# A graph layer on one core: six kept units fetched row by row by SyncE, ten by POOL

## The chip, the cores and the metric

The kernel runs on one core of one Trainium2 chip. Times are device microseconds of one execution; a kernel's time is the median of its runs. The trace is of one more execution, taken by the hardware profiler. Engines are named as in the profile: PE is the matrix engine (TensorE), PEld its weight load, DVE the vector engine, ACT the scalar engine, POOL GpSimd, and SP SyncE, which here only issues transfers (SPq is its queue of instructions).

## The reference

There are 6250 nodes with 256 features and 206,250 edges, sorted by their target `dst`. All is fp32.

```python
h = relu(layernorm(x))
e = relu(raw @ W_e1.T + b_e1) @ W_e2.T + b_e2            # raw: 64 numbers an edge
edge_emb = (e * (clip(polarity, 0, 1) + 0.01)) @ W_le.T + b_le
msg = relu(h[src] + edge_emb)                            # a row of h for each edge
aggr = segment_sum(msg, dst)
g = (h + aggr) @ W_g1.T + b_g1
out = x + relu(layernorm(g) * ln_g + ln_b) @ W_g2.T + b_g2
```

## The kernel before, in words

The edges are padded and cut into 806 units of 256 edges. Two units are a block; twelve units (`GU`) are a group of 3072 edges, of which there are 68. A buffer `hg` or `hx` (the latter eight lie in another tensor's memory) holds the 256 gathered rows of one unit: 128 partitions, two halves of 256 features.

The rows of the layer's input with its bias are first written to DRAM as `hb_d`. POOL gathers from there: one indirect DMA (L722) fetches 128 rows by the numbers in a column of `src_s`, two of them make a unit. Units are gathered in the order of a list, `order`, as buffers come free. There are 25 buffers (`HG`).

A loop runs over the units. For each unit `edge_part` lets TensorE form the edge products (L372); DVE multiplies them by the polarity and adds the gathered rows in place (`whole`, L755), and ACT applies the ReLU in place (L766). After the twelfth unit of a group three things follow: the first layer of edges to come (L338, fed by `raw` tiles that SP loads at L320), then the sums (`add_pairs`, L806: 96 matmuls that add up the rows of a group by target, using a selection matrix `sel`), and then `keep`: ACT and DVE copy the sum into a tile `ms` (L824, L825). A unit's buffer is free once its matmuls at L806 are done, and then POOL may gather into it the unit that comes 25 further on.

The first 24 units (`KEPT`, groups 0 and 1) are different. Their edge products are made at the start, while the layer's input is still being made, and kept in tiles `msg`. Units 0 to 7 (`RAW`) get rows straight from x, early. For units 8 to 23, the kernel before puts the gather into `order` ahead of unit 42 + 36 n, which is every third group, at its middle. One unit later, `whole_kept` (L770 to L787) multiplies, adds and applies the ReLU, and the product's buffer is free again at once, in the middle of the group. When a kept group's last unit is whole, `ready` names it and its sums are formed at the next group's end.

SP is a queue in program order too. A group's work on it: `raw` loads (L320), then `rows_out`, which loads four row numbers into SP's registers (L905) and stores the four strips of `ms` at these rows of `sum_d` in DRAM (L910); the load of `xt` (L240); the load of `ab`, the finished sums of 128 nodes (L943), which DVE adds to the nodes' rows some units later (L946); a clearing of rows of `sum_d` (L899) and the store of an output (L235). `soon(n, fn)` puts such a step n units later.

Of the kernel before, what the change touches and what calls it, by code (L numbers as in the profile page):

```python
# [10 lines left out]
I32 = mybir.dt.int32  # L11
# [6 lines left out]
P = 128  # L18
N = 6250
# [9 lines left out]
S = 4  # L29
L = 6  # L30
# [6 lines left out]
NP = -(-NB // 2)  # L37
# [3 lines left out]
LEAD = 22  # L41
BANKS = 8
RAW = 8
HG = 17 + RAW
GU = 2 * L
KEPT = 2 * GU
EVERY = 6 * L
SEEDS = 3
FILL = 3
FEW = KEPT // 4  # L50
# [23 lines left out]
def groups_of(w):  # L74
    return [g for g in range(NG) if w in windows_of(g)]
# [22 lines left out]


@with_exitstack  # L100
def gnn_kernel(ctx: ExitStack, tc: tile.TileContext, x, src_c, dst_c, dst_r, pol_c, raw_t, w_e1t, w_e2,
               w_let, w_g1t, w_g2t, vec_c, row_v, x_t, out):
    nc = tc.nc

# [2 lines left out]
    hb_d = dram.tile([N, D], F32, name="hb_d")  # L107
# [38 lines left out]
    def apart_from(ins, *others):  # L146

        for other in others:
            if other is not None:
                tc.declare_no_dep(ins.ins, other.ins, reason="what is waited for has waited for it")  # L150
# [100 lines left out]
    with fast:  # L251
# [8 lines left out]
        raw, fours, sel, e1, hg, msg, ms = {}, {}, {}, {}, {}, {}, {}  # L260
# [101 lines left out]
        def plain(u):  # L362

            return u < LEAD and u % 3 == 1
# [32 lines left out]
        def seed(u):  # L397

            if KEPT <= u < NU and u not in seeds:
                bank = ps.take(True, True)  # L400
                bank.held = True
                a = nc.scalar.activation(bank.tile, bc_s, AF.Copy)  # L402
                if bank.reader is not None:
                    apart_from(a, bank.writer)
                seeds[u] = bank
# [34 lines left out]
        def forward(u, between=lambda: None):  # L440

            edge_part(u)
            between()
            turn_of(u)
# [50 lines left out]
        with tc.tile_pool(name="p1", bufs=4) as p1, tc.tile_pool(name="p1x", bufs=11) as p1x:  # L495
# [76 lines left out]
            for k in range(len(parts) + 1):  # L572
# [24 lines left out]
                for _ in range((k > 0) + (k > 2 and k % 3 > 0)):  # L597
                    u = next(units, None)
                    if u is not None:
                        forward(u)  # L600
                if k in lists:
                    t, src = lists[k]
# [93 lines left out]
        with tc.tile_pool(name="hg", bufs=1) as hg_p, tc.tile_pool(name="ms", bufs=4) as ms_p, \  # L696
# [5 lines left out]
            free = deque((hg_p.tile([P, 2, D], F32, name=f"hg{i}"), ()) for i in range(RAW, HG))  # L702
            fetched = RAW
            order = list(range(KEPT, NU))
            beside = {}
            for r in range(RAW, KEPT):
                i = KEPT + EVERY * (r - RAW) + EVERY // 2
                beside[i] = r
                order.insert(order.index(i), r)
            order = deque(order)  # L710
# [5 lines left out]
            def gathers():  # L716

                while free and order:
                    u = order.popleft()
                    hg[u], formerly[u] = free.popleft()  # L720
                    for i in range(2):
                        g = nc.gpsimd.indirect_dma_start(  # L722
                            out=hg[u][:, i, :], out_offset=None, in_=hb_d,
                            in_offset=bass.IndirectOffsetOnAxis(ap=src_s[:, 2 * u + i:2 * u + i + 1], axis=0))
                        apart_from(g, *formerly[u])

            def select(g):

                return [(g, lambda k=k: rows_of_blocks(g, k)) for k in range(0, len(blocks_of(g)), 2)]
# [12 lines left out]
            def piece():  # L742

                due_now = [s for s in steps if s[0] <= now][:1]
                if due_now:
                    steps.remove(due_now[0])
                    due_now[0][1]()
                elif rest:
                    rest.popleft()[1]()

            def whole(u):

                bank = seeds.pop(u)
                for i in range(2):
                    product = nc.vector.scalar_tensor_tensor(  # L755
                        hg[u][:, i, :], bank.tile[:, i, :], pol_s[:, 2 * u + i:2 * u + i + 1], hg[u][:, i, :],
                        op0=ALU.mult, op1=ALU.add)
                    apart_from(product, *formerly[u])
                    users.setdefault(u, []).append(product)
                    if u == NU - 1:  # L760
                        nc.scalar.activation(hg[u][:, i, :], hg[u][:, i, :], AF.Relu)
                bank.reader = product
                bank.held = False
                ps.touch(bank)
                if u < NU - 1:
                    done[u] = product, nc.scalar.activation(hg[u], hg[u], AF.Relu)  # L766
                    apart_from(done[u][1], *formerly[u])
                    users[u].append(done[u][1])

            def whole_kept(u):  # L770

                m = msg[u]
                if u < RAW:
                    nc.vector.tensor_add(hg[u], hg[u], ble_b.rearrange("p (o d) -> p o d", o=1).to_broadcast([P, 2, D]))
                if plain(u):
                    nc.vector.tensor_add(m, m, bc_s)
                for i in range(2):
                    nc.vector.scalar_tensor_tensor(m[:, i, :], m[:, i, :], pol_s[:, 2 * u + i:2 * u + i + 1],  # L778
                                                   hg[u][:, i, :], op0=ALU.mult, op1=ALU.add)
                nc.scalar.activation(m, m, AF.Relu)  # L780
                free.append((hg[u], ()))
                hg[u] = m
                u += 1
                if u % (2 * L) == 0:
                    g = u // (2 * L) - 1
                    rest.extend(select(g))
                    ready.append(g)  # L787

# [92 lines left out]
            late = {}  # L881
            steps = deque()
            rest = deque()
            ready, fillers = [], []
            left = {w: set(groups_of(w)) for w in range(NW) if groups_of(w)[-1] < FAR}
            held_back = sorted(left)[-FILL:]
# [2 lines left out]
            moves = {}  # L889
# [192 lines left out]
            def due():  # L1082

                fns = todo.pop(now, deque())
                if fns and not (KEPT <= now < NF * GU and now % GU in QUIET):
                    fns.popleft()()
                if fns:
                    todo.setdefault(now + 1, deque()).extendleft(reversed(fns))

            gathers()  # L1090
            sums = add_pairs

# [26 lines left out]
            raw_at = {}  # L1119
# [12 lines left out]
            for u in range(LEAD, NU):  # L1132
                now = u

                def between():

                    nonlocal made
                    for n in range(1, SEEDS + 1):
                        if u + n <= u // GU * GU + GU:
                            seed(u + n)  # L1140
                    piece()
                    if KEPT <= u:
                        whole(u)
                        made += 1
                    r = raw_at.get(u, beside.get(u - 1))
                    if r is not None:
                        whole_kept(r)

                forward(u, between)
                for n in range(1, SEEDS + 1):  # L1150
                    seed(u + n)
                gathers()
                due()
                for fn in moves.pop(now, []):
                    fn()
                if len(rest) + len(steps) > 4:
                    piece()
                if u == NU - 24:
                    for w in range(NW):
                        if groups_of(w)[-1] == NG - 1:  # L1160
                            late[w] = node_work(w, True)
                if u == LEAD + 60:
                    flag = nc.values_load(bad_i[0:1, 0:1], min_val=0, max_val=4 * P)
            while todo:
                now = min(todo)
                for fn in todo.pop(now):
                    fn()
            assert not moves
            while steps:
                steps.popleft()[1]()  # L1170
            (_, _, h_rows, h_one, h_normed, h_two, h_three, _), = ending[-2]
# [205 lines left out]
```

## Time and profile before

| | us |
|---|---|
| median of three runs | 3826.62 |
| lowest, highest | 3807.94, 3829.58 |
| the profiled execution | 3820.48 |
| its span, first to last instruction | 3818.7 |
| mean granted TensorE clock | 0.789 |
| busy: PE, POOL, DVE, ACT | 3030.0, 1563.9, 1315.3, 1295.4 |
| idle of ACT ahead of L824, which copies a sum | 1791.0 |

A row of groups gives the line, engine, operation and tiles, the count, then the busy time and the mean of one in ns, and then the idle time of the engine ahead of them with what ended most of it. A row of waits gives who waited, for whom, then the time in total, how often, and the longest. A row of the timeline gives start and length, engine, line, operation, count, and in brackets the idle time ahead and its releaser. A row that begins with a stretch of time (`720.00:730.00`) gives what each engine did in it. A row of one line's instructions gives the count, then shortest, median and longest in ns, and the first and last start.

Over the span the picture repeats with the group, 57 us on average: TensorE is busy without a gap for about half of it, and the other half goes with the sums.

### The profile page before, as it was taken

The page shows a single profiled execution, that of the slowest core. Times are in us where ns is not written, and L with a number is a line of the kernel's source. Part 1 is how long each engine was busy: PE and PEld are TensorE (multiplying, and loading weights), DVE is VectorE, ACT ScalarE, POOL GpSimd, SP SyncE. Part 2 cuts the span into 40 slices and gives each one's busy share as a digit, 9 for nine tenths or more (in the row PEclk, how much of TensorE's full clock was granted, in tenths as well). Part 3 has the DMA queues.
Part 4 walks back from the last instruction along what each step waited for, and adds up shares of the span by engine and source line. Part 5 has one row for each costly group of instructions (what it writes and reads, how often), then busy time and mean ns, then how long its engine had stood idle before and what let it go on. Part 6 is the DMA issues. An engine that isn't in the chain of part 4 may idle for free.

```text
span 3818.7 us, 51854 instructions
## 1 busy us (share of the span) xinstructions
PE 3030.0 (79%) x19998; PEld 1840.7 (48%) x19998; DVE 1315.3 (34%) x2970; ACT 1295.4 (34%) x2408; POOL 1563.9 (41%) x1674
## 2 busy tenths in 40 slices
PE   8477787788787787788787788787787888787788
PEld 5344454454455454454455455455454455455446
DVE  5343233242233232233233233233233343233234
ACT  5243233243233232333233233233242343233234
POOL 7434434424434434434433434433434434433431
PEclk9787787787787787787787787787787787787788
DMA  7322222223223222223322222322222222222321
GB/s 252 103 74 81 83 85 84 84 74 92 87 79 89 85 81 79 83 79 90 90 82 77 86 80 83 95 82 73 89 82 88 83 82 81 86 82 79 88 76 44
DMA packets 143718, 331.53 MB, mean 87 GB/s; under 512 B 36000, under 2 KB 71417, under 8 KB 142713
## 3 DMA queue, kind: packets, MB, share of 16 engines
q0 software_dynamic: 77376, 211.39, 19.2%
q1 hardware_dynamic: 64788, 113.47, 9.7%
q8 instruction: 159, 2.61, 0.3%
q10 hardware_dynamic: 1300, 3.29, 0.3%
q14 instruction: 95, 0.77, 0.1%
HBM read 306.25 MB, written 34.08 MB: 89 GB/s over the span
## 4 chain that ended last, share of the span: by engine, by line
PE 66%; another core or an unknown queue 16%; issue 14%; DVE 2%; ACT 2%; DMA 1%; POOL 0%; DVEq 0%; ACTq 0%; POOLq 0%
PE pz L372 41%; PE pz L806 13%; PE pz L338 9%; PE pz L188 1%; PE pz L227 1%; PE pz L173 1%; DVE hg L755 1%; ACT hg L766 1%; ACT pz L402 0%; PE pz L214 0%; ACT ms L824 0%; DVE sel L737 0%; DVE msg L778 0%; DMA hg<-hb_d,src_s 0%
## 5 line engine op out<-in xcount | busy, mean ns | idle before, releaser
L372 PE MATMUL pz<-wc_s,e 128*128 128x256 f32 x6448 | 1857.5, 439 | 407.0 <-issue 331.4
L372 PEld LDWEIGHTS pz<-wc_s,e 128*128 128x128 f32 x6448 | 1387.7, 220 | 861.4 <-issue 589.3
L722 POOL DMA_INDIRECT hg<-hb_d,src_s x1096 | 1038.3, 947 | 1394.3 <-PE pz L806 856.6
L722 POOL DMA_INDIRECT hx<-hb_d,src_s x500 | 473.6, 947 | 789.5 <-PE pz L806 461.3
L825 DVE TENSOR_TENSOR ms<-ms,pz 128x256 f32<-128x256 f32 x68 | 28.7, 421 | 1842.9 <-remote 715.0
L806 PE MATMUL pz<-hg,sel 64*32 64x256 f32 x4312 | 520.6, 406 | 174.7 <-issue 147.1
L824 ACT ACTIVATE ms<-pz 128x256 f32<-128x256 f32 x68 | 26.0, 383 | 1791.0 <-remote 1700.4
L755 DVE SCALAR_TENSOR_TENSOR hg<-pz,pol_s,hg 128x256 f32<-128x256 f32 x1078 | 467.4, 479 | 352.9 <-PE pz L372 90.2
L766 ACT ACTIVATE hg<-hg 128x512 f32<-128x512 f32 x538 | 337.7, 628 | 401.3 <-DVE hg L755 351.8
L402 ACT ACTIVATE pz<-bc_s 128x512 f32<-128x512 f32 x782 | 453.2, 586 | 0.0
L806 PEld LDWEIGHTS pz<-hg,sel 64*32 64x32 f32 x4312 | 164.8, 108 | 487.9 <-issue 457.8
L338 PE MATMUL pz<-raw,we_s 64*32 64x512 f32 x6448 | 377.5, 596 | 7.8 <-DVE hg L755 5.0
L350 DVE TENSOR_SCALAR e<-pz,vecs 128x512 f32<-128x512 f32 x395 | 296.3, 751 | 106.3 <-remote 24.6
L806 PE MATMUL pz<-hx,sel 64*32 64x256 f32 x1944 | 263.4, 407 | 82.5 <-issue 71.7
L353 ACT ACTIVATE e<-pz,vecs 128x512 f32<-128x512 f32 x411 | 272.6, 683 | 96.3 <-PE pz L338 40.5
L755 DVE SCALAR_TENSOR_TENSOR hx<-pz,pol_s,hx 128x256 f32<-128x256 f32 x486 | 211.8, 479 | 161.0 <-PE pz L372 49.7
L338 PEld LDWEIGHTS pz<-raw,we_s 64*32 64x32 f32 x6448 | 116.4, 107 | 226.5 <-issue 127.0
L766 ACT ACTIVATE hx<-hx 128x512 f32<-128x512 f32 x243 | 152.6, 628 | 189.9 <-DVE hx L755 165.8
L806 PEld LDWEIGHTS pz<-hx,sel 64*32 64x32 f32 x1944 | 81.1, 108 | 230.1 <-issue 217.3
L173 PE MATMUL pz<-ident,stb 128*128 128x128 f32 x84 | 25.6, 403 | 84.5 <-issue 63.9
L737 DVE SCALAR_TENSOR_TENSOR sel<-iota_w,zero_c,rel 128x256 f32<-128x256 f32 x202 | 92.6, 477 | 0.0
L173 PEld LDWEIGHTS pz<-ident,stb 128*128 128x128 f32 x84 | 13.4, 196 | 105.3 <-issue 79.5
(136 smaller groups left out, 741.8 us busy)
## 6 DMA issues: line engine op xcount, KB each, us to landing
raw<-in_raw_t_dram SPq DMA_DIRECT2D x99, 512.0 KB
hg<-hb_d,src_s POOLq DMA_INDIRECT x1096
sum_d<-zero_d SPq DMA_DIRECT2D x47, 256.0 KB
ab<-sum_d SPq DMA_DIRECT2D x42, 256.0 KB
sum_d<-ms SPq DMA_DIRECT2D x264, 32.0 KB
hx<-hb_d,src_s POOLq DMA_INDIRECT x500
hb_d<-hb SPq DMA_DIRECT2D x12, 512.0 KB
xt<-in_x_dram SPq DMA_DIRECT2D x11, 512.0 KB
```

What stands on the lines that cost most here:

```text
L173: z = nc.tensor.transpose(pt[:, 0, c * P:c * P + n], a[:n, c * P:(c + 1) * P], ident[:n, :n])
L188: z = nc.tensor.matmul(ph[:n, 0, :], aT[:, c, :n], wg1_s[:, c, :], start=c == 0 and not bias_by_pe, stop=c == 1)
L338: z[c] = nc.tensor.matmul(bank[s, c].tile[j * W:(j + 1) * W].rearrange("p a b -> p (a b)"), we1_s[s * F:(s + 1) * F, c * P + j * W:c * P + ...
L350: a = nc.vector.tensor_scalar(e1[b][:, c, :], pe, be1_s[:, c:c + 1], 0.0, op0=ALU.add, op1=ALU.max)
L353: a = nc.scalar.activation(e1[b][:, c, :], pe, AF.Relu, bias=be1_s[:, c:c + 1])
L372: z = nc.tensor.matmul(bank.tile[:, i, :], e1[b][:, c, k:k + P], wc_s[:, c, :], start=not seeded and i == c == 0, stop=c == 1, skip_group_ ...
L402: a = nc.scalar.activation(bank.tile, bc_s, AF.Copy)
L722: g = nc.gpsimd.indirect_dma_start(out=hg[u][:, i, :], out_offset=None, in_=hb_d, in_offset=bass.IndirectOffsetOnAxis(ap=src_s[:, 2 * u + ...
L737: nc.vector.scalar_tensor_tensor(sel[g][:, k * S:k * S + n, :], iota_w.rearrange("p (o w) -> p o w", o=1).to_broadcast([P, n, W]), zero_c, ...
L755: product = nc.vector.scalar_tensor_tensor(hg[u][:, i, :], bank.tile[:, i, :], pol_s[:, 2 * u + i:2 * u + i + 1], hg[u][:, i, :], op0=ALU. ...
L766: done[u] = product, nc.scalar.activation(hg[u], hg[u], AF.Relu)
L806: z = nc.tensor.matmul(acc[g][h][j * W:(j + 1) * W, :], sel[g][h * F:(h + 1) * F, k * S + j, :], m[h * F:(h + 1) * F, j % 2, :], start=k = ...
```

## The change

Of the sixteen kept units 8 to 23, the last ten are still gathered by POOL, ahead of unit 54 + 60 n: every fifth group. The first six are fetched by SP. Their row numbers come in a new input, `src_r`: 128 of them in a row for each half of a unit. `place_of_rows` takes one buffer from the free ones. At each even unit, `some_rows` loads six of the numbers into registers of SP (one TENSOR_LOAD) and issues six transfers of one row each (1 KB) from `hb_d` into the buffer; 22 calls make 128 rows, 44 a unit. When the last row is issued, `whole_kept` is set for six units later, and the buffer goes back; the next unit of the six takes one. In all there are 264 register loads, 1536 row transfers and twelve loads of lists; POOL has twelve gathers fewer, 1584 for 1596. Since the kept units no longer become whole in their order, a group now counts its whole units (`whole_units`). The sums of kept group 0 are formed at about group 35 now (group 12 before), those of kept group 1 at about group 51 (48 before).

```diff
-EVERY = 6 * L
+EVERY = 5 * GU
+ROWS = 6
+BY_ROW = 6
...
-            for r in range(RAW, KEPT):
-                i = KEPT + EVERY * (r - RAW) + EVERY // 2
+            for n, r in enumerate(range(RAW + BY_ROW, KEPT)):
+                i = KEPT + EVERY * n + EVERY // 2
                 beside[i] = r
                 order.insert(order.index(i), r)
...
+            single = deque((r, i) for r in range(RAW, RAW + BY_ROW) for i in range(2))
+            listed = {}
+            at_row = 0
+
+            def numbers(k):
+
+                if k < len(single) and single[k] not in listed:
+                    r, i = single[k]
+                    listed[r, i] = nk.tile([1, P], I32, name=f"list{i}")
+                    nc.sync.dma_start(out=listed[r, i], in_=src_r[2 * r + i:2 * r + i + 1, :])
+
+            def place_of_rows(u):
+
+                if u > LEAD + 40 and single and single[0][0] not in hg and free:
+                    hg[single[0][0]] = free.popleft()[0]
+
+            def some_rows(u):
+
+                nonlocal at_row
+                if not single:
+                    return
+                r, i = single[0]
+                if r not in hg:
+                    return
+                if at_row == 0:
+                    numbers(0)
+                    numbers(1)
+                n = min(ROWS, P - at_row)
+                _, found = nc.values_load_multi_w_load_instructions(
+                    listed[r, i][0:1, at_row:at_row + n], engines=[mybir.EngineType.SP], min_val=0, max_val=N - 1,
+                    skip_runtime_bounds_check_because="a row of a node")
+                for k in range(n):
+                    p = at_row + k
+                    nc.sync.dma_start(out=hg[r][p:p + 1, i, :], in_=hb_d[bass.ds(found[k], 1), :])
+                at_row += n
+                if at_row == P:
+                    at_row = 0
+                    single.popleft()
+                    if i == 1:
+                        v = u + 6
+                        while v in raw_at or v - 1 in beside:
+                            v += 1
+                        raw_at[v] = r
...
-                u += 1
-                if u % (2 * L) == 0:
-                    g = u // (2 * L) - 1
+                g = u // GU
+                whole_units[g] = whole_units.get(g, 0) + 1
+                if whole_units[g] == GU:
                     rest.extend(select(g))
                     ready.append(g)
...
+                place_of_rows(u)
                 gathers()
+                if u > LEAD + 40 and u % 2 == 0:
+                    some_rows(u)
```

SP's queue is what the change moves most. Before, in a group of the middle of the program, this stands on SP between the load of edges (L320) and the load of finished sums (L943):

```order
L320 DMA raw<-in_raw_t_dram 128x1024 x2
L905 TENSOR_LOAD base_i
L910 ISA
L910 DMA sum_d<-ms 32x256
...
L240 DMA xt_7020<-in_x_dram 128x256
...
L910 DMA sum_d<-ms 32x256
L943 DMA ab<-sum_d 128x512
```

Nothing lies between the edges and the stores of the sum, nor between the last store and the load of sums. In the same group of the changed program the first of these places reads as follows on SP (its lines are numbered higher: L322 is L320 of before, L952 is L905, L957 is L910, L242 is L240, L990 is L943; L757 and L762 are the new ones):

```order
L322 DMA raw<-in_raw_t_dram 128x1024 x2
L757 TENSOR_LOAD list_6541
L762 ISA
L762 DMA hg_868<-hb_d 1x256
...
L952 TENSOR_LOAD base_i
L957 ISA
L957 DMA sum_d<-ms 32x256
```

One call of six rows has come between them (the line of dots stands for the other five). The second place, still on SP, in the same group:

```order
L957 DMA sum_d<-ms 32x256
L757 TENSOR_LOAD list_6541
L762 ISA
L762 DMA hg_868<-hb_d 1x256
...
L990 DMA ab<-sum_d 128x512
L757 TENSOR_LOAD list_6541
...
L762 DMA hg_868<-hb_d 1x256
```

The load of sums has moved behind one call of six rows. Four more calls follow it up to the next load of edges. PE, ACT and DVE have as many instructions as before.

More of the change, by code (lines that the diff above doesn't have):

```diff
@@ L100, in gnn_kernel @@
 @with_exitstack
-def gnn_kernel(ctx: ExitStack, tc: tile.TileContext, x, src_c, dst_c, dst_r, pol_c, raw_t, w_e1t, w_e2,
+def gnn_kernel(ctx: ExitStack, tc: tile.TileContext, x, src_c, src_r, dst_c, dst_r, pol_c, raw_t, w_e1t, w_e2,
                w_let, w_g1t, w_g2t, vec_c, row_v, x_t, out):
@@ L883, in gnn_kernel @@
             rest = deque()
+            whole_units = {}
             ready, fillers = [], []
@@ L1167, in gnn_kernel @@
                     fn()
-            assert not moves
+            assert not moves and not single and not ready
             while steps:
@@ L1353 @@
         "src_c": edge_cols(src, 0),
+        "src_r": padded(tiles(src, 0), NP * 2 * S, 0),
         "dst_c": edge_cols(dst, N),
```

## The prediction

> **What bounds the kernel now.** I read the page first: the busy shares, the chain that ended last, then the groups.
>
> ```profile
> PE 3030.0 (79%) x19998; PEld 1840.7 (48%) x19998; DVE 1315.3 (34%) x2970; ACT 1295.4 (34%) x2408; POOL 1563.9 (41%) x1674
> PE 66%; another core or an unknown queue 16%; issue 14%; DVE 2%; ACT 2%; DMA 1%; POOL 0%; DVEq 0%; ACTq 0%; POOLq 0%
> L722 POOL DMA_INDIRECT hg<-hb_d,src_s x1096 | 1038.3, 947 | 1394.3 <-PE pz L806 856.6
> L722 POOL DMA_INDIRECT hx<-hb_d,src_s x500 | 473.6, 947 | 789.5 <-PE pz L806 461.3
> ```
>
> TensorE carries the chain. The gathers, the work that the change touches, have 0% of it, and POOL's idle time ahead of them ends when TensorE's sums (L806) give a buffer back. But an average over the span says nothing of stages, so I next took four stretches of one group and the timeline around them.
>
> ```profile
> 720.00:730.00 10.00, 10.00 (x48) 8.72 (x46) 7.74 (x19) 6.50 (x12) 2.15 (x2) 1.00 0.09 27
> 730.00:739.00 9.00, 8.80 (x194) 3.83 (x192) 5.77 (x9) 5.55 (x10) 0.00 (x0) 1.00 0.38 118
> 750.00:760.00 10.00, 5.91 (x13) 2.65 (x13) 0.00 (x0) 0.00 (x0) 7.57 (x9) 0.50 0.37 107
> 780.00:790.00 10.00, 10.00 (x49) 8.79 (x48) 5.96 (x17) 7.25 (x15) 0.00 (x0) 1.00 0.22 66
> ```
>
> (Columns: length, busy time and instructions of PE, its weight load, DVE, ACT and POOL, then granted clock, DMA share, GB/s.) A group has two parts. In the fast one (720 to 739, 780 to 790) TensorE is full at a clock of 1.00. In the slow one (750 to 760) it does 13 matmuls in ten microseconds at 0.50, ACT and DVE stand still, and POOL gathers.
>
> ```profile
> 735.39 3.46 PE L806 MATMUL pz<-msg,sel 64*32 64x256 f32 x96
> ACT ms L824 <- remote: 1700.4, 60, 32.6
> 725.49 1.21 POOL L722 DMA_INDIRECT hg<-hb_d,src_s  x1 [14.91 <-ACT hg L766]
> 727.00 0.95 POOL L722 DMA_INDIRECT hg<-hb_d,src_s  x1 [0.30 <-DVE stb L946]
> 740.45 0.94 POOL L722 DMA_INDIRECT hg<-hb_d,src_s  x1 [12.50 <-PE pz L806]
> 741.70 0.94 POOL L722 DMA_INDIRECT hg<-hb_d,src_s  x1 [0.30 <-issue]
> ```
>
> The 96 matmuls that sum a kept group, whose buffers no gather waits for, took 3.46 us. The 96 of an ordinary group hold ACT for 1700.4 / 60 = 28.3 us: some 25 us more, with POOL issuing a gather every 741.70 - 740.45 = 1.25 us. So the slow part is paced by gathers, 24 to a group, and is about half of the time. I don't know from these rows by what mechanism.
>
> **The change, part by part.** *Twelve gathers less.* What a gather costs depends on its part of the group. Those of 725.49 and 727.00, which a kept unit brings, stand in the window of 720 to 730, where TensorE is busy 10.00 of 10.00: free. I checked this over many groups by windows from a group's start to the next one's.
>
> ```profile
> 884.94:939.50 54.56, 45.18 (x300) 27.85 (x300) 18.94 (x42) 19.23 (x37) 24.73 (x27) 0.78 0.28 83
> 2593.96:2650.46 56.50, 43.94 (x288) 26.49 (x288) 18.20 (x39) 18.79 (x34) 23.75 (x26) 0.77 0.27 78
> sum 627.70, PE 500.61 PEld 302.06 DVE 213.70 ACT 212.79 POOL 265.01; mean PE 45.51 PEld 27.46 DVE 19.43 ACT 19.34 POOL 24.09
> 939.50:992.00 52.50, 42.47 (x289) 25.72 (x288) 17.50 (x37) 17.93 (x33) 22.84 (x25) 0.79 0.31 91
> sum 620.45, PE 496.34 PEld 299.70 DVE 203.75 ACT 206.49 POOL 244.06; mean PE 45.12 PEld 27.25 DVE 18.52 ACT 18.77 POOL 22.19
> 2534.23:2593.96 59.73, 47.29 (x306) 28.67 (x304) 18.23 (x40) 18.73 (x35) 27.36 (x29) 0.79 0.30 88
> sum 685.46, PE 543.94 PEld 329.47 DVE 221.05 ACT 224.21 POOL 285.27; mean PE 45.33 PEld 27.46 DVE 18.42 ACT 18.68 POOL 23.77
> ```
>
> The first sum is of eleven groups that hold a kept unit's two gathers (first and last shown): 57.06 us each. The second is of the eleven that follow them. The third is of eleven more without kept gathers, with the group of 52.50 counted once again: (620.45 + 685.46 - 52.50) / 22 = 56.97. The two gathers cost 0.1 us, and since single groups lie between 52.5 and 60 us, that is nothing to within about 1 us. Bounds for the twelve: nothing, or their full price of 1.25 us, 15 us. I take nothing: they are of the kind just compared.
>
> *1536 row fetches on SyncE, with 264 loads of six numbers into its registers.* The nearest rows are the stores at L910, also addressed by a register, and the load of their addresses.
>
> ```profile
> L910 SPq DMA_DIRECT2D sum_d<-ms x264: 314/322/699, 168.1 to 3774.1; - x132
> L910 SPq FUSED_REGOPS  x264: 42/46/698, 154.4 to 3773.0; - x132
> L910 SPq MOVE sum_d<-ms x264: 3/29/363, 154.7 to 3773.1; - x132
> L905 SPq TENSOR_LOAD <-base_i x66: 295/300/505, 153.8 to 3747.5; - x66
> 779.68 0.36 SPq L943 DMA_DIRECT2D ab<-sum_d  x1
> 780.08 0.50 SPq L899 DMA_DIRECT2D sum_d<-zero_d  x1
> 783.25 4.77 SPq L910 DMA_DIRECT2D sum_d<-ms  x4
> ```
>
> Medians: 0.32 + 0.05 + 0.03 = 0.40 us, and three gaps between neighbours of 780.08 - 779.68 - 0.36 = 0.04: 0.52 us. That is the low end. The four stores at 783.25 each wait until the one before has landed: (4.77 - 0.32) / 3 = 1.48 us, the high end. A row fetch waits in the order only for a transfer issued eight earlier, so I take 0.55. A call of six rows is 0.30 + 0.04 + 6 x 0.55 = 3.6 us. Most groups hold six calls: 22 us. The kernel has 67 groups and the fetches lie in 47 of them.
>
> The Trainium skill speaks against this part: "DMA: Bandwidth & Descriptors", "Rules for kernel authors", wants many small transfers made into one large one, since below 64 KB one pays mostly overhead; a row is 1 KB. By the rows above that overhead is SyncE's and not the path's, so the sum stays; what it does when SyncE has no room is the first rival.
>
> What is hidden behind? SyncE's own waits say where it has room.
>
> ```profile
> SPq L910 <- DVE ms L825: 884.8, 31, 33.4
> SPq L320 <- PE pz L338: 507.7, 65, 40.1
> SPq L235 <- DVE ot L232: 493.4, 41, 15.0
> SPq L910 <- DMA sum_d<-ms: 122.2, 116, 2.9
> 797.79 0.36 SPq L320 DMA_DIRECT2D raw<-in_raw_t_dram  x1
> 786.94 0.42 DVE L946 TENSOR_TENSOR stb<-stb,ab 128x256 f32<-128x256 f32 x1
> 771.62 0.38 ACT L824 ACTIVATE ms<-pz 128x256 f32<-128x256 f32 x1 [32.57 <-remote]
> ```
>
> One call stands between the load of the edges (L320) and the stores of a sum (L910). There SyncE waits for the sum anyway, 884.8 / 31 = 28.5 us, so that call is covered and whatever SyncE is late by is made good here in every group. The others stand behind the stores. There SyncE now waits 493.4 / 41 = 12.0 us for an output and 507.7 / 65 = 7.8 us for the first layer, 20 us in all; the five calls need 18. What overflows goes into the 28.5. Its own work is about 9 us (from 771.62 to 780.58), so 31 of 57 us are filled. The edges that L320 loads are needed a group later: some microseconds cost nothing.
>
> *What is queued behind them.* Behind one call stands the load of the sums (L943), and DVE's addition (L946) waits for that. Now it is issued at 779.68 and used at 786.94: 7.26 us. The longest wait for a landing in the row above is 2.9 us, which I take as an estimate for this load too. There remain 7.26 - 2.9 - 3.6 = 0.8 us: nothing waits, though it is near. The first row of a unit also waits for its buffer, which a sum released before: SyncE's cover again. Six small list loads more are noise of the same kind.
>
> *The transfers themselves.* Do more transfers slow TensorE?
>
> ```profile
> 772.49 1.89 SPq L910 DMA_DIRECT2D sum_d<-ms  x2
> 774.43 1.45 SPq L240 DMA_DIRECT2D xt<-in_x_dram  x1
> 776.71 1.79 SPq L910 DMA_DIRECT2D sum_d<-ms  x2
> 773.00:789.00 16.00, 16.00 (x68) 13.71 (x68) 10.11 (x27) 10.53 (x22) 0.00 (x0) 0.88 0.23 67
> 712.00:728.00 16.00, 16.00 (x68) 13.76 (x68) 10.87 (x27) 11.28 (x21) 2.15 (x2) 0.90 0.14 39
> ```
>
> From 773 to 789 SyncE issued ten transfers (with those at 779.68, 780.08 and 783.25), from 712 to 728 four at the same lines; both windows hold 68 matmuls. I take nothing. What they can't see is one matmul, 16 / 68 = 0.24 us, for six transfers: for 36 rows that is at most 1.4 us a group, 66 us over 47 groups. A store there moves 32 KB, a row fetch 1 KB, so the truth should lie far below that end.
>
> *One buffer of 25 held for the rows.* POOL runs ahead until it meets a buffer that a sum hasn't released; with 24 it meets it a unit earlier, and a sum of twelve units still releases twelve. A group's next gathers come over 30 us before use. I take nothing. The kept sums are formed at other groups, 3.46 us each as now.
>
> The sum: 3820.5 us (the profiled execution, span 3818.7) + 0, from -15 to +66. The median of the runs is 6 us above that execution, so I state **3824 us**, between the two. A measurement of this kernel tells about 1% (38 us) from no change.
>
> **The rivals.**
>
> *SyncE becomes late (slower).* The place is the load at L943. If a row takes over (7.26 - 2.9 - 0.34) / 6 = 0.67 us, DVE waits, and behind it the edge products that TensorE's banks wait for. For it: my 0.55 stands near it. Against: rows need not wait for each other's landing, and the cover behind a late SyncE is 28.5 us. At 1.48 us a call is 9.2 us, six are 55, with SyncE's own 9 that makes 64 us against a group of 57: +7 x 47 = 330 us, 4150 us. Just past 0.67 the loss is a microsecond or two in 42 groups: 3870 to 3910 us.
>
> *Row fetches pace the sums as gathers do (slower).* One call, six rows, falls at the head of the slow part. If each row fetch held TensorE there as a gather does, 1.25 us, that is 6 x 1.25 x 47 = 350 us: 4170. It decides from 38 / (6 x 47) = 0.13 us a row. For it: nobody knows from the trace why a gather paces the sums, and both read the same array. Against: the edge loads and stores that SyncE issues leave TensorE at 1.00.
>
> *The gathers' price counts (faster, inside 1%).* If every gather costs 1.25 us wherever it stands, 3820.5 - 15 = 3806 us. The comparison of groups speaks against it. The Trainium skill has such a rule in "Perfetto Trace Analysis", "DMA Optimizations": where the making of descriptors is the bottleneck, spreading transfers over the engines that can issue them may help.
>
> *The sums fall otherwise (faster).* Groups differ by 59.73 - 52.50 = 7.2 us, and the short one has 25 POOL operations where the long one has 29: how many gathers meet the sum decides. With other buffers in another order the mix may change. If ten more of the 60 groups became short: -72 us, 3750 us. Nothing in the trace says which way the mix goes.
>
> **How the numbers follow.** The forecast (nothing measurable) has 0.55. The full price of the gathers has 0.08 and is within 1% too: 0.63. A late SyncE has 0.12 and fetches that pace the sums 0.15: slower 0.27. Another mix of sums has 0.10: faster. The upper half of the transfers' bound (over +38) is counted with the second rival. The likeliest case's own range is 3806 to 3858 (-15 to +38). The range takes in the whole bound of the transfers (3887), the mild form of a late SyncE and half of another mix: 3785 to 3890 us.
>
> **What would show it.** Right: the gathers number 12 fewer; a row fetch in the trace costs SyncE about 0.55 us; SyncE's wait for the sum (28.5 us) shrinks by a few microseconds and stays over 15; L946 still waits for nothing; the fast windows keep 48 or 49 matmuls in 10 us; and the mean wait of L824 stays at 28. Wrong: waits at L946 for the load of sums, a wait of L824 that is longer by several microseconds in the 47 groups with rows alone, or fast windows under 47 matmuls.

## The result and the profile after

The changed kernel took 3870.0 us (3864.4 to 3880.4, four runs), the kernel before 3828.1 us beside it: 1.0123 times as long, 95% interval 1.0081 to 1.0165. That is 42 us against a forecast of no change. Run twice more beside the experiments, where the kernel before took 3867.2 and 3865.4 us, it took 1.0158 (1.0123 to 1.0193) and 1.0103 (1.0068 to 1.0139) of that. The ratios compare the fast runs of both kernels alone, so they can differ a little from the quotient of two medians. The profiled execution took 3864.4 us, its span is 3862.6.

The page of the changed kernel, with the rows that answer to those of before (L724 is L722 of before, L852 is L806):

```profile
PE 3035.2 (79%) x19998; PEld 1851.8 (48%) x19998; DVE 1314.1 (34%) x2970; ACT 1296.0 (34%) x2408; POOL 1552.5 (40%) x1662
PE 59%; another core or an unknown queue 24%; issue 11%; DVE 2%; ACT 2%; SPq 0%; POOL 0%; DMA 0%; DVEq 0%; ACTq 0%; POOLq 0%
L724 POOL DMA_INDIRECT hg<-hb_d,src_s x1072 | 1015.4, 947 | 1661.8 <-PE pz L852 1157.5
L724 POOL DMA_INDIRECT hx<-hb_d,src_s x512 | 485.1, 947 | 577.9 <-PE pz L852 293.4
```

Twelve gathers are gone, and TensorE is busy only 5 us longer. But POOL waits longer for the sums to release buffers: 1157.5 + 293.4 = 1450.9 us, where it was 856.6 + 461.3 = 1317.9. (All of its idle time ahead of gathers rose by less, from 2183.8 to 2239.7 us.) SyncE's part, from the instructions of its new lines (shortest, median, longest in ns) and its waits:

```profile
L762 SPq DMA_DIRECT2D hg<-hb_d x1536: 2/228/1363, 334.4 to 2944.8; - x192
L757 SPq TENSOR_LOAD <-list x264: 387/982/1724, 333.3 to 2943.4; - x132
L993 DVE TENSOR_TENSOR stb<-stb,ab 128x256 f32<-128x256 f32 x84 | 34.8, 415 | 0.0
```

```profile
SPq L957 <- DVE ms L871: 691.7, 28, 33.1
SPq L322 <- PE pz L340: 238.5, 41, 40.4
SPq L237 <- DVE ot L234: 84.2, 8, 15.5
```

Two thirds of the time that SyncE had to spare in the fast part are used up: its waits for an output fell from 493.4 to 84.2 us, those for the first layer from 507.7 to 238.5. Yet nobody waits for it: the addition that uses the load of sums (L993, L946 of before) still has 0.0 us of idle time ahead of it.

What the rows do shows in one sum. First POOL and SyncE in the kernel before, in a group whose sums begin at 799.20:

```profile
816.36 0.95 POOL L722 DMA_INDIRECT hg<-hb_d,src_s  x1 [0.30 <-issue]
817.61 0.94 POOL L722 DMA_INDIRECT hx<-hb_d,src_s  x1 [0.30 <-issue]
818.86 0.95 POOL L722 DMA_INDIRECT hx<-hb_d,src_s  x1 [0.30 <-issue]
820.87 0.94 POOL L722 DMA_INDIRECT hg<-hb_d,src_s  x1 [1.07 <-remote]
```

And in the changed kernel, in a group whose sums begin at 1424.53:

```profile
1420.13 2.33 SPq L762 DMA_DIRECT2D hg<-hb_d  x6
1426.32 3.35 SPq L762 DMA_DIRECT2D hg<-hb_d  x6
...
1439.16 0.95 POOL L724 DMA_INDIRECT hx<-hb_d,src_s  x1 [0.30 <-issue]
1440.41 0.95 POOL L724 DMA_INDIRECT hx<-hb_d,src_s  x1 [0.30 <-issue]
1442.70 0.94 POOL L724 DMA_INDIRECT hx<-hb_d,src_s  x1 [1.34 <-remote]
```

A gather follows the last one after 1.25 us as long as released buffers lie ready. In the first group POOL runs dry for the first time after 16 gathers (800.11 to 818.86), in the second after 13 (1425.43 to 1440.41), and there six rows went out at 1426.32 to 1429.67, in the first microseconds of the sums. I counted this in all ordinary groups between 300 and 2900 us of the span: POOL runs dry after 17.6 gathers on average before, after 13.6 in the change. A window of ten microseconds from the start of these two sums says the same of TensorE (first row before, second row the change):

```profile
799.20:809.20 10.00, 7.94 (x95) 2.60 (x79) 0.96 (x2) 0.83 (x2) 6.96 (x8) 0.91 0.39 126
```

```profile
1424.50:1434.50 10.00, 6.68 (x84) 2.46 (x69) 0.99 (x2) 0.86 (x2) 6.93 (x8) 0.81 0.56 179
```

95 matmuls are done in the sum without rows, 84 in the one with them. The waits of TensorE's weight loads within the sums, of before and then of the change, show the same over the whole span:

```profile
PEld pz L806 <- issue: 676.2, 848, 2.0
```

```profile
PEld pz L852 <- issue: 919.4, 1060, 2.6
```

These waits grew by 243 us, but the kernel lost only 42. Most of them are hidden, since a sum's copy comes well after its last matmul. In the group whose sums begin at 799.20, before:

```profile
817.09 0.58 PE L806 MATMUL pz<-hg,sel 64*32 64x256 f32 x1 [1.46 <-issue]
829.90 0.38 ACT L824 ACTIVATE ms<-pz 128x256 f32<-128x256 f32 x1 [29.70 <-remote]
```

So the 28.3 us for which "the 96 of an ordinary group hold ACT" are not the time of the 96 matmuls: these were over some 12 us before the copy. (The profile gives "remote" for what the copy waits for, which names no engine.) In the change ACT waits as long as ever:

```profile
ACT ms L870 <- remote: 1515.8, 53, 31.3
```

That is 28.6 us each. Over the 45 ordinary groups counted, the matmuls of a sum take 21.5 us from the first to the last in place of 15.1, but the copy follows the first matmul after 29.5 us in place of 29.9.

What a group loses by it isn't the same in each. From the starts of ACT's ReLUs, groups 4 to 50 together took 2692.8 us before and 2727.0 now: 34 of the 42 us. Of that 21 us lie between the first and the last unit of a group and 13 between a group's last unit and the next one's first. Groups with a short slow part (under 36 us by that measure) fell from 17 to 12. A split of the 45 groups at the copy shows more. In 32 of them, before as now, the copy comes over 29 us after the first matmul, and from sums to sums such a group takes 59.0 us before and 58.9 now: nothing is lost there. In the other 13, before as now, the copy comes early; these took 53.8 us and now take 56.2. There TensorE does 31 matmuls between 8 and 18 us after the copy, where it did 45.5 (47 in the late groups, before and now). So what these groups lose is lost where a sum ends early, in the fast part behind it. An example is at 1214 us, where a sum of 22.5 us is followed by a fast part of 25.4 (19.2 is the usual; fast parts of over 22 us rose from none to 7):

```profile
1221.50 0.94 POOL L724 DMA_INDIRECT hg<-hb_d,src_s  x1 [0.30 <-issue]
1224.60 1.13 PE L190 MATMUL pz<-wg_s,hT 128*128 128x256 f32 x4 [3.78 <-ACT hT L179]
1219.00:1229.00 10.00, 6.22 (x22) 4.88 (x21) 3.58 (x10) 4.09 (x9) 2.83 (x3) 0.85 0.34 99
```

Gathers run back to back until 1222.44, and TensorE waits 3.78 us for ACT just behind them. Why the fast part suffers so isn't shown: before, five or six gathers stood behind an early copy too.

### The profile page after: what moved, and what is told of

It is laid out like the page before. It is cut to its first block, busy times and chain, and to the rows that moved or that the text cites. A ratio compares the mean times of both kernels' runs of the same rounds, so it can differ in the third digit from the quotient of the medians.

```text
span 3862.6 us, 56941 instructions
## 1 busy us (share of the span) xinstructions
PE 3035.2 (79%) x19998; PEld 1851.8 (48%) x19998; DVE 1314.1 (34%) x2970; ACT 1296.0 (34%) x2408; POOL 1552.5 (40%) x1662
## 4 chain that ended last, share of the span: by engine, by line
PE 59%; another core or an unknown queue 24%; issue 11%; DVE 2%; ACT 2%; SPq 0%; POOL 0%; DMA 0%; DVEq 0%; ACTq 0%; POOLq 0%
PE pz L374 35%; PE pz L852 11%; PE pz L340 9%; PE pz L190 1%; PE pz L229 1%; DVE hg L801 1%; ACT hg L812 1%; PE pz L175 1%; ACT pz L404 0%; PE pz L216 0%; ACT ms L870 0%; DVE sel L783 0%; SPq L762 0%; POOL hg L724 0%
## 5 line engine op out<-in xcount | busy, mean ns | idle before, releaser
L374 PE MATMUL pz<-wc_s,e 128*128 128x256 f32 x6448 | 1723.7, 426 | 230.3 <-issue 142.5
L724 POOL DMA_INDIRECT hg<-hb_d,src_s x1072 | 1015.4, 947 | 1661.8 <-PE pz L852 1157.5
L374 PEld LDWEIGHTS pz<-wc_s,e 128*128 128x128 f32 x6448 | 1372.3, 216 | 573.4 <-issue 256.6
L852 PE MATMUL pz<-hg,sel 64*32 64x256 f32 x4240 | 618.7, 432 | 269.3 <-issue 240.5
L724 POOL DMA_INDIRECT hx<-hb_d,src_s x512 | 485.1, 947 | 577.9 <-PE pz L852 293.4
L870 ACT ACTIVATE ms<-pz 128x256 f32<-128x256 f32 x68 | 26.0, 383 | 1760.0 <-remote 1515.8
L801 DVE SCALAR_TENSOR_TENSOR hg<-pz,pol_s,hg 128x256 f32<-128x256 f32 x1060 | 459.2, 478 | 427.2 <-PE pz L374 118.8
L852 PEld LDWEIGHTS pz<-hg,sel 64*32 64x32 f32 x4240 | 180.5, 111 | 671.4 <-issue 640.4
L852 PE MATMUL pz<-hx,sel 64*32 64x256 f32 x2016 | 294.0, 421 | 125.3 <-issue 112.0
L852 PEld LDWEIGHTS pz<-hx,sel 64*32 64x32 f32 x2016 | 89.5, 110 | 291.3 <-issue 278.4
L190 PE MATMUL pz<-wg_s,hT 128*128 128x256 f32 (+1 forms) x176 | 51.7, 419 | 43.3 <-ACT hT L179 36.4
```

The source lines that it names most:

```text
L190: z = nc.tensor.matmul(ph[:n, 0, :], aT[:, c, :n], wg1_s[:, c, :], start=c == 0 and not bias_by_pe, stop=c == 1)
L374: z = nc.tensor.matmul(bank.tile[:, i, :], e1[b][:, c, k:k + P], wc_s[:, c, :], start=not seeded and i == c == 0, stop=c == 1, skip_group_ ...
L724: g = nc.gpsimd.indirect_dma_start(out=hg[u][:, i, :], out_offset=None, in_=hb_d, in_offset=bass.IndirectOffsetOnAxis(ap=src_s[:, 2 * u + ...
L801: product = nc.vector.scalar_tensor_tensor(hg[u][:, i, :], bank.tile[:, i, :], pol_s[:, 2 * u + i:2 * u + i + 1], hg[u][:, i, :], op0=ALU. ...
L852: z = nc.tensor.matmul(acc[g][h][j * W:(j + 1) * W, :], sel[g][h * F:(h + 1) * F, k * S + j, :], m[h * F:(h + 1) * F, j % 2, :], start=k = ...
```

## The experiments

Three theories. **H** (head): rows that go out while sums are formed delay TensorE's releases. **B**: the held buffer and the new places of the kept gathers shift the mix of long and short groups. **F**: the rows slow the fast part. The first four kernels ran side by side on one chip, where the kernel before took 3827.1 us.

**No call at the head.** The call between the loads of edges and the stores of the sum goes to the group's middle:

```diff
-                if u > LEAD + 40 and u % 2 == 0:
+                if u > LEAD + 40 and u % 2 == 0 and u % GU:
                     some_rows(u)
+                    if u % GU == GU // 2:
+                        some_rows(u)
```

> All 1536 rows are still fetched, but the call that stood between the load of edges and the stores of the sum is issued at the group's middle, as a second call there; so no row moves while the sums are formed. Theory H (head: six row transfers in the first 5 us of the sums delay TensorE's releases of buffers, POOL runs dry sooner, more groups take the long form of about 59 us in place of about 53): the time falls back to 3820 to 3840 us, and groups whose slow part is under 36 us are 15 or more of groups 4 to 50 again (17 before, 12 in the change). Theory B (the held buffer and the other places of the kept gathers shift the mix): stays at 3860 to 3880. Theory F (30 to 36 rows in the fast part slow TensorE or the vector engines): 3870 or a few us more, since all 36 now lie there.

It took 1.0173 (1.0103 to 1.0242) of the kernel before: against H, it seemed. But the trace shows that rows had not left the sums. SyncE, and TensorE's first matmuls of the same sums:

```profile
1412.95 16.30 SPq L762 DMA_DIRECT2D hg<-hb_d  x24
1430.45 2.10 SPq L322 DMA_DIRECT2D raw<-in_raw_t_dram  x2
```

```profile
1420.94 1.25 PE L852 MATMUL pz<-hg,sel 64*32 64x256 f32 x34
```

The sums begin at 1420.94 and SyncE issues rows until 1429.25: 36 rows don't fit into the fast part beside its other work. Counted from a microsecond ahead of a sum's first matmul on, 6.0 rows a group still go out there (7.1 in the change); from the first matmul on, 4.7 (6.5). The edit didn't do what it was to do, and decides nothing between H and F.

**No rows at all.** One transfer of 128 rows for each half unit:

```diff
-                _, found = nc.values_load_multi_w_load_instructions(
...
-                for k in range(n):
-                    p = at_row + k
-                    nc.sync.dma_start(out=hg[r][p:p + 1, i, :], in_=hb_d[bass.ds(found[k], 1), :])
+                if at_row == 0:
+                    nc.sync.dma_start(out=hg[r][:, i, :], in_=hb_d[0:P, :])
```

> The six kept units are filled by one transfer of 128 consecutive rows for each half, in place of 128 rows at their own numbers (so the rows are not the listed ones): 12 transfers and no register loads, with the buffer held just as long and the kept gathers of POOL at the places of the change. Theory H and theory F: 3810 to 3835 us, as before the change or a little under. Theory B: 3860 to 3880 us, as the change.

0.9966 (0.9918 to 1.0013): B falls. POOL runs dry after 17.5 gathers, and 17 groups have a short slow part, as before.

**Six rows at the head, alone**, in the kernel before:

```diff
+                if LEAD + 40 < u < 50 * GU and u % GU == 0:
+                    for k in range(6):
+                        p = (u * 6 + k) % P
+                        nc.sync.dma_start(out=spot[p:p + 1, :], in_=hb_d[p:p + 1, :])
```

> The kernel before, with nothing of the change but six added transfers of one row (1 KB, fixed addresses, into a tile that nobody reads) between the load of edges and the stores of the sum, in groups 5 to 49. Theory H: slower than before by 20 to 50 us (3850 to 3880), with the first releases of the sums later, between 3 and 9 us after their start. Theories B and F: no change, 3815 to 3840 us.

1.0109 (1.0063 to 1.0154): 42 us from 264 transfers of 1 KB that nobody reads. **Thirty rows behind the stores, alone**, the same four lines with `u % 2 == 0 and u % GU`:

> The kernel before, with 30 added transfers of one row a group (fixed addresses, into a tile that nobody reads) behind the stores of the sum, none ahead of them. Theory F: slower by 25 us or more (3853 and up). Theories H and B: no change, 3815 to 3840 us.

1.0000 (0.9960 to 1.0040): F falls for rows at fixed addresses. The weight loads' waits within the sums, for six at the head and then for thirty behind it:

```profile
PEld pz L807 <- issue: 795.0, 949, 2.6
```

```profile
PEld pz L807 <- issue: 666.5, 831, 2.0
```

POOL runs dry after 16.5 gathers in the first and 17.6 in the second. In the first, the matmuls of a sum take 21.5 us in the 20 groups in which all six rows go out behind the first matmul, and 16.2 us in the 22 in which two do; but from sums to sums these groups take the same, 58.4 and 58.5 us. Short slow parts number 10 in the first and 15 in the second, against 17: again the loss shows in the mix and not in the groups that the rows delay most.

**What makes a row dear, and a version without rows in the sums.** Four kernels ran side by side: the change with four kept units by rows in four calls a group (`BY_ROW = 4`, `EVERY = 4 * GU`, `u % GU in (2, 4, 6, 8)`), twelve rows at the head, one transfer of six rows at the head, and the kernel before with its loads of edges moved behind the stores of the sum.

> The change with four kept units fetched by SyncE in place of six (1024 rows; POOL gathers twelve, every fourth group) in four calls a group behind the stores of the sum, at the units 2, 4, 6 and 8 of it: 4 x 3.5 + 9 = 23 us of SyncE's work in a fast part of 27, so that no row is left over for the sums. (With the call at the head moved to the middle, SyncE was late and 6.0 rows a group still went out while the sums were formed.) Theory H (rows during the sums delay TensorE's releases): 3800 to 3835 us, and POOL issues some 17.5 gathers before its first gap, as before the change (13.6 in the change). If rows cost wherever they lie, or register loads do: 3850 us or more.

> The kernel before with twelve added one-row transfers at the head of the sums in place of six. Theory H, by number: the first gap of POOL comes after about 15.4 gathers (17.6 with none, 16.5 with six), and the time is 3870 to 3900 us. If the mere presence of some transfers decides: as with six, 3860 to 3875 and 16.5.

> The kernel before with one added transfer of six rows at the head of the sums in place of six transfers of one row: the same bytes. If the number of transfers counts (each ends with its own report to a semaphore, which TensorE's reports wait behind): 3820 to 3840 us and a first gap after 17.4 gathers or more. If bytes or descriptors of a row count: 3855 to 3880 us and 16.5.

> The kernel before with its loads of edges (one or two of 512 KB a group) moved from the head of the sums to the sixth unit of the next group, behind the stores of the sum. Theory H in its wide form (every transfer at the head delays the releases): POOL issues more gathers before its first gap than 17.6, and the time falls by 10 us or more. If only transfers that are many count: no change, 3815 to 3840 us, 17.6.

They fell on a chip on which the kernel before took 2118.8 us. The ratios are 1.0006 (0.9997 to 1.0016), 0.9998 (0.9989 to 1.0008), 0.9992 (0.9981 to 1.0002) and 1.0015 (1.0006 to 1.0025): nothing to lengthen, nothing lengthened, and all four expectations of a difference missed for want of the slow part. Windows of the first of them, across a whole sum:

```profile
720.00:730.00 10.00, 10.00 (x190) 5.82 (x196) 6.62 (x11) 5.71 (x10) 7.56 (x9) 1.00 0.63 179
730.00:740.00 10.00, 10.00 (x69) 8.48 (x55) 5.53 (x14) 5.98 (x12) 7.56 (x9) 1.00 0.57 177
```

```profile
PEld pz L852 <- issue: 22.3, 72, 1.3
```

POOL gathers as fast as ever (9 in ten microseconds) and TensorE runs on beside it: 22.3 us of such waits in place of 676.2. So the slow part that I took for a property of the program depends on the chip that it ran on, or on its state then: each chip of the experiments was used in one session. Three of the four were run again, with the change itself, on a chip where the kernel before took 3867.2 us.

> The change itself, unaltered, run beside the three others below. The four runs before this one fell on another chip, on which the kernel before took 2118.8 us in place of 3827: there the sums of a group took 3.2 us, with the gathers going on beside them, in place of 28.7. Where the kernel before takes about 3830 us, the change takes 3860 to 3880. Where it takes about 2118 us, theory H (rows delay the releases of buffers in the slow sums) expects no change, 2112 to 2126 us, since there is no slow part to lengthen; a cost of the rows of their own would show as 2130 us or more.

> The kernel with four kept units fetched by SyncE in four calls a group behind the stores of the sum, once more. Where the kernel before takes about 3830 us: theory H 3800 to 3835 and some 17.5 gathers before POOL's first gap; if rows cost wherever they lie, 3850 or more. Where it takes 2118 us: 2118 again.

> Twelve one-row transfers at the head of the sums of the kernel before, once more. Where the kernel before takes about 3830 us: theory H by number, a first gap after about 15.4 gathers and 3870 to 3900 us. Where it takes 2118 us: 2118 again.

> One transfer of six rows at the head of the sums of the kernel before, once more. Where the kernel before takes about 3830 us: if the number of transfers counts, 3820 to 3840 us and a first gap after 17.4 gathers or more; if bytes or descriptors count, 3855 to 3880 us and 16.5. Where it takes 2118 us: 2117 again.

The change: 1.0158. Twelve rows at the head: 1.0223 (1.0185 to 1.0261), 86 us, twice the six. One transfer of six rows: 1.0036 (1.0002 to 1.0070), at the edge of nothing. The weight loads' waits, twelve and then one:

```profile
PEld pz L807 <- issue: 1009.1, 1084, 2.7
```

```profile
PEld pz L807 <- issue: 853.5, 916, 2.7
```

POOL runs dry after 14.2 and 16.2 gathers. (On this chip some 16 is the value without rows: 16.05 in the version with none in the sums, though that isn't the kernel before, of which there is no trace here.) So it seems to be the number of transfers that counts, not their bytes. That agrees with the Trainium skill ("DMA: Bandwidth & Descriptors", "Rules for kernel authors": many small transfers are better made into one), though the price here is TensorE's and not the queue's. One rival is left: the single transfer goes out where the first of the six would, about 1.0 us ahead of the sums' first matmul or 0.7 us behind it, while the six reach up to 2.5 us into the sums. Whether one transfer put deeper into the sums would cost more was not tried. The version with no rows in the sums took 1.0077 (1.0024 to 1.0129), which H did not expect; its trace has no row in the sums and still only 7 short slow parts. Its parts were taken one by one on a further chip (kernel before 3846.0 us), with the loads of edges moved as a fourth:

> The version with 24 rows a group and none in the sums (1.0077 of the kernel before when last run), but each row fetched from a fixed address (so the rows are not the listed ones), with no loads of SyncE's registers. If what is left of the cost comes from the register loads (1.0 to 1.2 us each, 0.3 expected): 0.995 to 1.004 of the kernel before. If it comes from the row transfers in the fast part: 1.005 or more.

> The same, but all 176 register loads are kept and only one row of each call is fetched by its number (4 a group in place of 24), the others by one transfer of 128 consecutive rows for each half (so most rows are not the listed ones). Register loads at fault: 1.005 or more. Row transfers at fault: 0.995 to 1.004.

> The same layout (a buffer held, four kept units filled by SyncE, twelve by POOL) with no row transfers and no register loads at all: one transfer of 128 consecutive rows for each half (so the rows are not the listed ones). If only rows and loads cost: 0.99 to 1.003 of the kernel before, and the first gap of POOL as in the version with rows (16.05 gathers there). If the layout costs (the kept gathers at every fourth group, a buffer less): 1.005 or more.

> The kernel before with its loads of edges (512 KB each) moved from the head of the sums to behind the stores of the sum, on a chip on which the sums are slow. One transfer of six rows at the head cost 0.4% at most, six transfers 1.1%, twelve 2.2%, so what counts is how many. One or two fewer at the head: 0.993 to 0.999. If bytes at the head counted too: 0.985 or less.

0.9985 (0.9950 to 1.0021), 1.0015 (0.9983 to 1.0047), 0.9993 (0.9967 to 1.0020) and 1.0022 (0.9993 to 1.0051): none of them shows a cost (the intervals end at 1.0051 at most), and moving the loads of edges gains nothing, where 0.993 to 0.999 was expected. (Their traces have 10 to 17 fast parts of over 22 us with no row in the sums, so on this chip long fast parts are no mark of rows.) Last, the whole version and the change side by side, with more runs, on a chip where the kernel before took 3865.4 us:

> The version with four kept units by rows (24 rows a group, at their own numbers, behind the stores of the sum, none in the sums), a third time and with more rounds, beside the change. Its parts alone were free: rows from fixed addresses 0.9985, register loads with four rows 1.0015, the layout 0.9993. If rows outside the sums are free (theory H alone): 0.997 to 1.004 of the kernel before. If rows and register loads together load SyncE so far that they cost: 1.005 to 1.012, as the first time (1.0077).

> The change itself beside it, with as many rounds: 1.012 to 1.017 of the kernel before, and POOL's first gap after 12.5 to 14 gathers; the difference to the version with none in the sums is what the rows in the sums cost: about 0.011 if theory H has all of it, 0.006 if it has half.

1.0019 (0.9987 to 1.0051) and 1.0103 (1.0068 to 1.0139). Their weight loads' waits:

```profile
PEld pz L852 <- issue: 826.6, 918, 2.7
```

```profile
PEld pz L852 <- issue: 955.5, 1054, 2.6
```

With rows in the fast part alone nothing is lost that can be told from noise; with rows in the sums too, 0.8% more, and POOL runs dry after 13.1 gathers in place of 16.2; short slow parts number 16 and 10. (The change also fetches six kept units in place of four, 36 rows a group in place of 24.) The 1.0077 didn't come back, and stays unexplained. No version gained against the kernel before, so none is proposed.

## Why the prediction was wrong, point by point

- **The step that failed: "What overflows goes into the 28.5", and of the call at the head, "so that call is covered"; with it the term "The transfers themselves", put at nothing.** I looked for cover on SyncE's queue alone. SyncE has that time, but the rows that it issues there are not free to TensorE. What I had to price was a transfer during the sums, and my row for "the transfers themselves" (68 matmuls in both windows) came from the fast part, where the answer is indeed nothing: 30 rows, 1.0000. I also took the truth to lie far below the end of 66 us because a row moves 1 KB and a store 32; but six rows in one transfer cost 0.4% or nothing, and six transfers 1.1%. At the head of the sums 264 rows cost 42 us, 0.16 us each on average. The change has 7.1 rows a group there, in 46 groups: 42 / (46 x 7.1) = 0.13 us each. This is a mean over groups of which most lose nothing.
- **The second rival had the place and, roughly, the price from which it decides** (0.13 us a row), and it had a chance of 0.15. Its own price, a gather's 1.25 us, is near what the rows do to TensorE's matmuls, (21.5 - 15.1) / 6.5 = 1.0 us a row. But it took all of that for lost (+350 us), and most is hidden ahead of the copy: the kernel lost an eighth. The trace of before held the warning: what paces the sums was unexplained there, and anything new put into an unexplained stage should not be booked at nothing. My argument against it, that loads and stores of SyncE leave TensorE at 1.00, again came from the fast part.
- **Twelve gathers at nothing: not settled.** With all else of the change and no rows, 0.9966 (0.9918 to 1.0013). That holds nothing as well as the full 15 us, which would be 0.9961.
- **SyncE's work: right in sum, wrong in its parts.** A row takes (2.33 - 0.23) / 5 = 0.42 us, not 0.55, and the load of six registers 0.98, not 0.30: 3.5 us a call against my 3.6. Its wait for the sum shrank to 691.7 / 28 = 24.7 us.
- **The first rival: refuted** at the place that it names. SyncE is late, but the load of sums is not waited for: 0.0 us ahead of L993.
- **The buffer held for the rows: right** (0.9966, 0.9993).
- **The mix of sums**, my rival on the faster side, did shift, but the other way: short slow parts fell from 17 to 12. With several rows in the sums the traces have 10 to 13 of them, without rows there 15 to 21, save the version of 1.0077 with 7; so the rows account for the shift in the main. Each count is from one execution.
- **The signs: most of those named for "right" came, and the time was still longer.** There are twelve gathers fewer, L946 (L993 now) waits for nothing, SyncE's wait for the sum is 24.7 us, and the mean wait of L824 (L870 now) is 28.6 against 28.3. The sign for "wrong" that did come is fast windows under 47 matmuls: 22 in the window at 1219, and 31 on average behind the 13 early copies.
- **The range** of 3785 to 3890 us holds the 3870; it did so by the bounds of the slower cases, not by the forecast.

What stays open: by what path a small transfer, or a gather, delays TensorE's signals during the sums; the runs show only that it goes by number, or by how far the transfers reach into the sums, and not by bytes. Nor is it shown how the delay of the matmuls, which the usual group hides, turns early sums into late ones and slows the fast part behind early copies. It also stays open why chips differ.

## What to carry to other kernels

A queue with spare time is not cover by itself: ask what its transfers do to the stage that they fall in, and take the price from that stage, not from a neighbouring one in which everything runs at full clock. A wait that grows is not yet time lost: ask what the next step waits for, and compare whole groups before and after. Where a stage is paced by something that you can't explain, small added transfers there deserve a price of their own, and one larger transfer is safer than six small ones. And when an edit is to take work out of a stage, check in its trace that the work has left: here a late queue carried it back.

## What the runs showed that I had not expected

- The same program takes 2118.8 us on one chip and 3827 to 3867 us on the four others that the experiments ran on. On the first, gathers and sums run beside each other; on the others the sums stall while gathers go on, and 1700 us go with that. An edit's worth can't be carried from one to the other: twelve rows at the head cost 2.2% on one chip and nothing (0.9998) on another.
- At the head of the sums, six one-row transfers cost 1.1%, twelve 2.2% (on another chip), and one of six rows 0.4% or nothing.
- Rows in the sums stretch TensorE's matmuls from 15.1 to 21.5 us in a group, and in 32 of 45 groups none of it reaches the time.
- A load of six registers from a row of a list took SyncE 0.98 us (up to 1.72), a load of four at L905 0.30.
